# A fused attention and recurrent block: another order of TensorE's work in the attention rounds

## The chip, the cores and the metric

The kernel runs on one core of a Trainium2 chip. The metric is the time of one execution on the device in microseconds. TensorE (PE) multiplies and transposes, VectorE (DVE) and ScalarE (ACT) work on what TensorE leaves in PSUM, GpSimd (POOL) and SyncE (SP) mostly issue transfers. Each engine has its own queue of instructions, and engines wait for each other by semaphores.

## The reference

The input is x of 4 x 1024 x 1024 in float32. It is normalized over its last axis (no gain, no offset), and goes two ways, whose results are multiplied:

- Attention: queries of 16 heads, keys and values of 4 heads, 64 wide. A query sees the 512 keys up to its own position and, besides, the first four keys of the sequence (the sinks). Softmax, weighted values, a last product with Wo.
- A recurrent FFN: the last token of each sequence is normalized, passed through one layer, then four times through (norm, 1024 to 4096, gelu, 4096 to 1024, add), then through one more layer. The result is added to every token under a sigmoid gate, normalized and passed through silu.

```
att = jnp.einsum('bkgqd,bkjd->bkgqj', q, k) * scale
att = jnp.where(mask[None, None, None, :, :], att, -jnp.inf)
att = jax.nn.softmax(att, axis=-1)
y = jnp.einsum('bkgqj,bkjd->bkgqd', att, v)
...
x = x + s * g
```

## The kernel before

There are three stages, one after the other: projections of x to queries, keys, values and gates (to about 1040 us), attention (to about 1974 us), and the output product with all that follows (to the end). The change touches attention alone.

**Rounds.** Attention works in 64 rounds. Query tiles of 128 rows come in pairs (`PAIRED`, L133): a far one (tiles 7 to 4 of a sequence), whose window is full, and a near one (tiles 0 to 3), which sees 1 to 4 key tiles. A pair takes four rounds, one for each two heads' pairs of queries; `Step` (L220) holds what one tile does in one round. So the near tile has 1 key tile for four rounds, then 2, 3 and 4, and this repeats for each of the four sequences.

**One step.** `scores` (L247) multiplies queries by keys on TensorE into S. S is one tile of four PSUM banks, with no second buffer. VectorE then puts the own keys where the window has moved on (L272, far alone), adds the mask, negates and takes the minimum (L289), ScalarE takes the exponential and the sum (L294). A far step's scores are taken for one of its two queries at a time (two calls), a near step's for both at once. `normalized` (L299) scales by the reciprocal sum on VectorE. `turned` (L307) transposes one tile of 128 keys for two heads and two queries: four transposes into a PSUM tile T, of which there are two, and a copy to pT by ScalarE (L316; four buffers). For a far tile 0 VectorE also makes `lead`, its part before the window's edge (L322). `turned_sinks` (L328) does the same for the four sink columns, in 32-column pieces. `values` (L349) multiplies a turned tile by v into yp, one PSUM bank with no second buffer; `values_apart` (L356) adds sinks and lead. `stored` (L368) copies yp out on VectorE, and every second time a transfer to memory follows.

**The FFN between.** The FFN has four columns of data and 1024 KB blocks of weights, so it is cut into 173 units, a generator from L652 on, and `filler(slot)` (L847) puts the units that are due into three places of each round. A unit is mostly one block: one load, and matmuls of 32 columns (L685). The last block of a stream is followed by a copy of the sums by VectorE (L691), and the next unit turns them by four transposes (L739) into the same T tiles, which VectorE adds up (L746, L747, L751).

**Order.** TensorE's order is written out by hand (`manual_schedule` with PE alone, L856): the calls in the loop of L857 stand in its queue as they are written. The other engines' orders are chosen by the scheduler when the kernel is built, from the waits between instructions. The scores of a round are those of the next round (`far_next`, `near_next`), so that VectorE and ScalarE have time for them.

Of the kernel before, what the change touches and what calls it, by code (L numbers as in the profile page):

```python
# [43 lines left out]
def recurrent_block_kernel(  # L44
# [92 lines left out]
    sink_values, leads = {}, {}  # L137

    def load_kv(b):

        pool = pools["odd" if b % 2 else "first"]
        kT = pool.tile([P, N_KV // 2, TT, P + SINK], F32, tag="kT", name=f"kT{b}")
        v = pool.tile([P, TT, KVD], F32, tag="v", name=f"v{b}")
        for h in range(TT // BLK):
            n, at = b * (TT // BLK) + h, slice(h * BLK, (h + 1) * BLK)
            for m in range(N_KV // 2):
                nc.sync.dma_start(
                    kT[:, m, at, SINK:], k_dram[n][:, m, :].rearrange("p (t k) -> p t k", k=P)
                )
            nc.sync.dma_start(v[:, at, :], v_dram[n])  # L150
        far = WINDOW // P
        nc.gpsimd.tensor_copy(
            kT[:, :, far:, :SINK],
            kT[:, :, 0:1, SINK : 2 * SINK].to_broadcast([P, N_KV // 2, TT - far, SINK]),
        )

        sinks = pools["first"].tile([P, PAIR, KVD], F32, tag="sinks", name=f"sinks{b}", bufs=2)
        nc.gpsimd.memset(sinks, 0.0)
        for g in range(2):
            for r in range(PAIR):  # L160
                end = (2 * g + r + 1) * QUAD
                nc.gpsimd.dma_start(
                    sinks[end - SINK : end, r, :].rearrange("p (m g c) -> p m g c", m=2, g=2)[
                        :, :, g, :
                    ],
                    v_dram[b * (TT // BLK)][:SINK, 0, :].rearrange(
                        "p (m g c) -> p m g c", m=2, g=2
                    )[:, :, g, :],
                )
        kTs[b], vs[b], sink_values[b] = kT, v, sinks  # L170

    def load_q(i):
        qTs[i] = pools["first"].tile([P, N_HEAD // 2, P], F32, tag="qT", name=f"qT{i}", bufs=4)
        n, j = divmod(i, BLK)
        nc.sync.dma_start(qTs[i], q_dram[n][:, :, j * P : (j + 1) * P])
# [44 lines left out]
    class Step:  # L220
# [132 lines left out]
            last = not self.far and k + 1 == len(self.keys)  # L353
            self.added(self.pT.pop(k), vs[self.b][:, self.keys[k], :], k == 0, last)

        def values_apart(self):  # L356

            for r in range(PAIR):
                for g in range(2):
                    cols = slice((2 * self.m + g) * HS, (2 * self.m + g + 1) * HS)  # L360
                    nc.tensor.matmul(  # L361
                        self.y[g * HS : (g + 1) * HS, r * P : (r + 1) * P],
                        sink_values[self.b][:, r, cols], self.sT,
                        start=False, stop=False, skip_group_check=True,
                    )
            self.added(self.lead, leads[self.i], False, True)

        def stored(self):  # L368
# [23 lines left out]
    def steps_of(tiles, m, rp):  # L392
        return [Step(i, m, rp) for i in tiles]
# [5 lines left out]
    with ExitStack() as a:  # L399
# [193 lines left out]
        for n in range(NBLK):  # L593
# [11 lines left out]
            for kind, w7, part in (  # L605
                (queries, wq7, 0), (queries, wq7, 1), (gates, wg7, 0), (gates, wg7, 1)
            ):
                if n == NBLK - 1 and kind is gates and part == 0:
# [8 lines left out]
                    far, near = steps_of(*order[0])  # L617
# [26 lines left out]
    with ExitStack() as a:  # L644
# [188 lines left out]
        def load_y(n, row):  # L833

            t = ws.tile([P, 2, KH, BT // 2], F32, tag="stream", name=f"y2_{n}_{row}")
            ys.setdefault(n, {})[row] = t
            for j in range(BLK // 2):
                nc.sync.dma_start(
                    t[:, :, :, j * P : (j + 1) * P],
                    y_dram[n * BLK + row * (BLK // 2) + j].rearrange(  # L840
                        "p (h c q) -> p h c q", h=2, c=KH
                    ),
                )
# [3 lines left out]
        def filler(slot):  # L847
            nonlocal ffn_done
            due = FFN_UNITS * (p * SLOTS + slot + 1) // (ffn_steps * SLOTS)
            while ffn_done < min(due, FFN_UNITS + 1):  # L850
                next(ffn_gen, None)
                ffn_done += 1

        with tc.manual_schedule(engines={mybir.EngineType.PE}):  # L856
            for p in range(len(order)):  # L857
                pair, within = divmod(p, per_pair)
                if within == 0:
                    b, t = divmod(pair, TT // 2)  # L860
                    i = PAIRED[pair][0]
                    own = i % TT
                    leads[i] = px.tile([P, KVD], F32, tag="leads", name=f"leads{i}", bufs=2)
                    nc.vector.tensor_tensor(
                        leads[i], vs[b][:, own - WINDOW // P, :], vs[b][:, own, :], ALU.subtract
                    )
                    if pair + 1 < len(PAIRED):
                        for i in PAIRED[pair + 1]:
                            load_q(i)
                    if t == 1 and b + 1 < B:  # L870
                        load_kv(b + 1)


                if 0 <= p - 2 * DT < 2 * DT:
                    c, g = divmod(p - 2 * DT, 2)
                    m, r = divmod(c, GROUP)
                    h = (2 * m + g) * GROUP + r
                    tc.keep_in_program_order(
                        nc.sync.dma_start(
                            wo_sb[g * HS : (g + 1) * HS, c, :],  # L880
                            wo[h // 4, h % 2 * HS : (h % 2 + 1) * HS,
                               h // 2 % 2 * D : (h // 2 % 2 + 1) * D],
                        )
                    )
                if p > 4 * DT:
                    for dst, minuend, subtrahend in islice(wo_parts, 1):
                        tc.keep_in_program_order(
                            nc.vector.tensor_tensor(dst, minuend, subtrahend, ALU.subtract)
                        )
                if p == ffn_steps:  # L890
                    for _ in ffn_gen:
                        pass
                    for row in range(2):
                        load_y(0, row)
                more = p + 1 < len(order)
                n_near = len(near.keys)
                far.turned(0)
                far.turned_sinks()
                if more:
                    far_next, near_next = steps_of(*order[p + 1])  # L900
                    far_next.scores((0,))
                for k in (1, 2):
                    far.turned(k)
                filler(0)
                for k in range(3):
                    far.values(k)
                far.turned(3)
                if more:
                    far_next.normalized((0,))
                    far_next.scores((1,))  # L910
                for k in range(min(2, n_near)):
                    near.turned(k)
                filler(1)
                far.values(3)
                far.values_apart()
                far.stored()
                for k in range(2, n_near):
                    near.turned(k)
                if more:
                    far_next.normalized((1,))  # L920
                    near_next.scores(both)
                for k in range(n_near):
                    near.values(k)
                if more:
                    near_next.normalized(both)
                near.stored()
                filler(2)
                if more:
                    far, near = far_next, near_next

# [275 lines left out]
```

## Time and profile before

| | us |
|---|---|
| median of 3 runs | 2368.65 (2368.1 to 2369.14) |
| profiled execution | 2368.6 |
| its span, first to last instruction | 2366.9 |
| TensorE busy | 2324.0 (98%) |
| VectorE busy | 1226.0 (52%) |
| ScalarE busy | 865.4 (37%) |
| TensorE busy within 1200 to 1600 us | 392.57 of 400 |
| VectorE, ScalarE within the same | 290.91, 246.62 |

Times are from the span's start. A line of the timeline gives start, duration, engine, line of the kernel, operation, tiles written and read, shape and count; in square brackets stands for how long the engine was idle before it, and what ended that. Durations of matmuls overlap, since they are pipelined, so the distance between starts tells what one costs. A line of groups gives the count, then busy time and the mean of one in ns, then the idle time of the engine ahead of it and its releaser. TensorE's granted clock was 1.00 in every stretch read.

### The profile page before, as it was taken

How to read it: one execution, taken by the hardware profiler on the slowest of the kernel's cores; microseconds unless marked ns; L12 is line 12 of the kernel's file. 1: busy time of each engine (PE TensorE's matmuls, PEld its weight loads, DVE VectorE, ACT ScalarE, POOL GpSimd, SP SyncE). 2: the span in 40 equal slices, each digit the busy share in tenths (PEclk: the TensorE clock that was granted, in tenths of full speed). 3: DMA queues.
4: the chain of work that ended last, by engine and by line, in shares of the span. 5: the costliest groups of instructions: out<-in, count | busy, mean ns of one | idle time of the engine just before them, and what ended most of it. 6: DMA issues, size and time to landing. Idle time of an engine off the chain costs nothing.

```text
span 2366.9 us, 31507 instructions
## 1 busy us (share of the span) xinstructions
PE 2324.0 (98%) x11966; PEld 1353.1 (57%) x11966; DVE 1226.0 (52%) x2973; ACT 865.4 (37%) x1960; POOL 322.9 (14%) x480
## 2 busy tenths in 40 slices
PE   7999999999999999999999999999999999999999
PEld 5757585757576666745555555555555554444444
DVE  7222222131212211147767767777777776777776
ACT  1110101010111111056666666666656664333332
POOL 2121313121212221320001000100000000111110
PEclk9999999999999999999999999999999999999999
DMA  8243111111111111346667777667466634667563
GB/s 338 96 172 125 62 59 62 45 72 49 60 52 66 49 54 40 112 157 210 201 199 233 249 218 227 204 213 231 155 215 219 215 89 165 176 192 201 153 170 89
DMA packets 190129, 348.79 MB, mean 147 GB/s; under 512 B 10789, under 2 KB 84597, under 8 KB 188441
## 3 DMA queue, kind: packets, MB, share of 16 engines
q1 hardware_dynamic: 161448, 252.74, 33.1%
q0 software_dynamic: 23200, 74.63, 10.3%
q10 hardware_dynamic: 5328, 19.40, 2.2%
q8 instruction: 94, 1.54, 0.3%
q14 instruction: 59, 0.48, 0.1%
HBM read 271.20 MB, written 92.31 MB: 154 GB/s over the span
## 4 chain that ended last, share of the span: by engine, by line
PE 80%; issue 14%; DVE 2%; ACT 2%; DMA 1%; POOL 1%; SPq 0%; ACTq 0%; POOLq 0%; DVEq 0%
PE u_q L538 16%; PE u L1044 15%; PE u_g L559 14%; PE S L267 6%; PE yp L344 6%; PE t L312 6%; PE kp L472 5%; PE vp L461 4%; PE d_ps L685 4%; PE xtp L450 1%; PE yp L361 1%; PE st L334 1%; DMA out_beta_sb<-in_out_beta_dram 1%; ACT pr L294 1%; POOL y_dram L379 0%
## 5 line engine op out<-in xcount | busy, mean ns | idle before, releaser
L294 ACT ACTIVATE pr<-pr,nm 128x516 f32<-128x516 f32 (+4 forms) x512 | 325.3, 639 | 137.8 <-DVE nm L289 137.1
L316 ACT COPY pT<-t 128x512 f32<-128x512 f32 x416 | 230.5, 585 | 218.1 <-PE t L312 216.8
L289 DVE CUSTOM_DVE_ANT_0 pr<-S,near_mask 128x516 f32<-128x516 f32 (+4 forms) x512 | 278.2, 590 | 36.7 <-PE S L267 32.1
L267 PE MATMUL S<-kT,qT 64*128 64x512 f32 (+4 forms) x1536 | 259.7, 456 | 2.7 <-DVE nm L289 2.7
L312 PE MATMUL t<-ident,pr 128*128 128x128 f32 x1664 | 245.0, 282 | 5.6 <-ACT pT L316 3.8
L312 PEld LDWEIGHTS t<-ident,pr 128*128 128x128 f32 x1664 | 177.5, 141 | 99.1 <-issue 68.1
L344 PE MATMUL yp<-pT,v 128*64 128x256 f32 x1664 | 222.4, 391 | 2.1 <-ACT pT L316 1.8
L305 DVE TENSOR_SCALAR pr<-pr,ri 128x516 f32<-128x516 f32 (+4 forms) x512 | 199.2, 437 | 5.9
L267 PEld LDWEIGHTS S<-kT,qT 64*128 64x128 f32 x1536 | 129.6, 186 | 118.6 <-issue 100.3
L344 PEld LDWEIGHTS yp<-pT,v 128*64 128x64 f32 x1664 | 101.8, 136 | 148.1 <-issue 68.3
L538 PE MATMUL u_q<-xT,wq_sb 128*128 128x256 f32 x768 | 172.2, 379 | 0.0
L559 PE MATMUL u_g<-wg_sb,xT 128*128 128x512 f32 x384 | 171.5, 592 | 0.0
L1044 PE MATMUL u<-wo_sb,y 128*128 128x512 f32 x384 | 170.1, 592 | 1.1 <-DVE y L374 1.1
L538 PEld LDWEIGHTS u_q<-xT,wq_sb 128*128 128x128 f32 x768 | 144.8, 190 | 22.5 <-issue 3.8
L451 ACT COPY xT<-xtp 128x512 f32<-128x512 f32 x64 | 37.5, 588 | 285.2 <-PE xtp L450 285.2
L379 POOL DMA_DIRECT2D y_dram<-y x64 | 35.6, 556 | 751.2 <-DVE y L374 735.8
L1044 PEld LDWEIGHTS u<-wo_sb,y 128*128 128x128 f32 x384 | 72.9, 190 | 92.9 <-issue 91.4
L559 PEld LDWEIGHTS u_g<-wg_sb,xT 128*128 128x128 f32 x384 | 71.8, 190 | 81.4 <-issue 80.6
L566 POOL TENSOR_TENSOR t_g<-t_g,gate_b_sb 128x512 f32<-128x512 f32 x64 | 87.1, 1361 | 195.8 <-DVE t_g L513 144.0
L538 PE MATMUL u_q<-s,wq_t 128*128 128x256 f32 x512 | 113.1, 379 | 0.0
L559 PE MATMUL u_g<-wg_t,s 128*128 128x512 f32 x256 | 112.7, 593 | 0.0
L461 PE MATMUL vp<-wv_sb,xT 128*128 128x256 f32 x512 | 112.6, 380 | 0.0
(198 smaller groups left out, 2971.3 us busy)
## 6 DMA issues: line engine op xcount, KB each, us to landing
d_w<-in_d_w_dram SPq DMA_DIRECT2D x128, 1024.0 KB, 5.9
xn<-in_x_dram ACTq DMA_DIRECT2D x34, 512.0 KB, 5.0
x<-in_x_dram SPq DMA_DIRECT2D x32, 512.0 KB, 3.9
q_dram<-t_q POOLq DMA_DIRECT2D x64, 256.0 KB, 2.6
g_dram<-t_g POOLq DMA_DIRECT2D x64, 256.0 KB, 2.3
qT<-q_dram SPq DMA_DIRECT2D x32, 512.0 KB, 4.8
y_dram<-y POOLq DMA_DIRECT2D x64, 256.0 KB, 4.3
y<-y_dram SPq DMA_DIRECT2D x32, 512.0 KB, 4.6
```

What stands on the lines that cost most here:

```text
L267: nc.tensor.matmul(S[:, dst, g, at_s], qTs[self.i][half[g], at + r, :], k, start=True, stop=True,)
L289: nc.vector.tensor_tensor_reduce(out=low, in0=S[:, src, g, :cols], in1=self.mask, scale=-1.0 / HS**0.5, scalar=-NEG, op0=ALU.add, op1=ALU.min,
L294: nc.scalar.activation(low, low, AF.Exp, bias=nm, scale=-1.0, accum_out=self.sums[:, r, g : g + 1],)
L305: nc.vector.tensor_scalar(at, at, rinv[:, r, g : g + 1], None, ALU.mult)
L312: nc.tensor.transpose(ps[:, g, r, :], self.pr[g][:, r, k * P : (k + 1) * P], ident)
L316: nc.scalar.copy(self.pT[k], ps.rearrange("p g r q -> p g (r q)"))
L344: nc.tensor.matmul(self.y[g * HS : (g + 1) * HS, :], v[:, cols], pT[:, g, :], start=first, stop=last,)
L461: nc.tensor.matmul(ps[:, h, :], xT[:, c, (j + h) * P : (j + h + 1) * P], wv_sb[:, c, :], start=(c == 0), stop=(c == DT - 1),)
L472: nc.tensor.matmul(ps, wk_sb[:, c, m * P : (m + 1) * P], xT[:, c, :], start=(c == 0), stop=(c == DT - 1),)
L538: nc.tensor.matmul(bank[:, h * (BT // 2) : (h + 1) * (BT // 2)], w7[i][:, c, at], left[n][i][:, c, :], start=(first and h == 0 and c == 0) ...
L559: nc.tensor.matmul(bank, left[n][i][:, c, j * P : (j + 1) * P], w7[i][:, c, :], start=(first and c == 0), stop=(c == KH - 1), skip_group_c ...
L1044: nc.tensor.matmul(bank, left[n][i][:, c, j * P : (j + 1) * P], wo7[i][:, c, :], start=(first and c == 0), stop=(c == KH - 1), skip_group_ ...
```

## The change

The order of TensorE's work within a round is changed; no computation is added or left out. Counting as one group what stands together in TensorE's queue with one shape of operands (transposes of keys, FFN blocks and sinks in 32 columns, scores, values):

- far tiles 0 and 1 are turned together ahead of the first scores, and tiles 2 and 3 together behind the sinks; before, tile 0 stood alone, 1 and 2 together, and 3 alone.
- the first filler goes ahead of the sinks, so that two groups of 32 columns meet.
- all far values, of tiles 0 to 3, sinks and lead, stand in one group ahead of the second query's scores; before, tiles 0 to 2 stood there ahead of turning tile 3, and the rest behind the second filler. `values_apart` is cut in two, with sinks ahead of tiles 2 and 3 and the lead last. `stored` moves along, ahead of the second scores.
- the third filler joins the second where the near tile has at most two key tiles.

```diff
-        def values_apart(self):
+        def sink_values(self):
...
+        def lead_values(self):
+
             self.added(self.lead, leads[self.i], False, True)
...
-                far.turned(0)
-                far.turned_sinks()
+                for k in (0, 1):
+                    far.turned(k)
                 if more:
                     far_next, near_next = steps_of(*order[p + 1])
                     far_next.scores((0,))
-                for k in (1, 2):
+                filler(0)
+                far.turned_sinks()
+                for k in (2, 3):
                     far.turned(k)
-                filler(0)
-                for k in range(3):
+                for k in range(2):
                     far.values(k)
-                far.turned(3)
+                far.sink_values()
+                for k in range(2, 4):
+                    far.values(k)
+                far.lead_values()
+                far.stored()
                 if more:
                     far_next.normalized((0,))
                     far_next.scores((1,))
                 for k in range(min(2, n_near)):
                     near.turned(k)
                 filler(1)
-                far.values(3)
-                far.values_apart()
-                far.stored()
+                if n_near <= 2:
+                    filler(2)
                 for k in range(2, n_near):
                     near.turned(k)
...
                 near.stored()
-                filler(2)
+                if n_near > 2:
+                    filler(2)
```

The instructions are the same in kind and number: 2431 rows of TensorE's order, 1455 of ScalarE's and 2958 of VectorE's in both. The orders of ScalarE and VectorE differ too, since the scheduler chooses them anew.

## The prediction

> **What bounds the kernel now.** I read the page first, then the timeline of two rounds in the attention stage (1040 to 1974 us of the span), then the groups with their releasers.
>
> ```profile
> span 2366.9 us, 31507 instructions
> PE 2324.0 (98%) x11966; PEld 1353.1 (57%) x11966; DVE 1226.0 (52%) x2973; ACT 865.4 (37%) x1960; POOL 322.9 (14%) x480
> L316 ACT COPY pT<-t 128x512 f32<-128x512 f32 x416 | 230.5, 585 | 218.1 <-PE t L312 216.8
> ```
>
> TensorE is busy 98%; nobody it waits for stands out. So the round is as long as TensorE's own list, and other engines' delays are hidden. One round, start, duration, engine:
>
> ```profile
> 1412.59 1.56 PE L267 MATMUL S<-kT,qT 64*128 64x384 f32 x8
> 1414.08 1.51 PE L344 MATMUL yp<-pT,v 128*64 128x256 f32 x12
> 1415.53 0.66 PE L312 MATMUL t<-ident,pr 128*128 128x128 f32 x4
> 1416.12 0.43 PE L334 MATMUL st<-ident,pr 128*32 128x128 f32 x8
> 1416.47 1.35 PE L267 MATMUL S<-kT,qT 64*128 64x512 f32 x8
> 1417.83 1.09 PE L312 MATMUL t<-ident,pr 128*128 128x128 f32 x8
> 1418.86 1.07 PE L685 MATMUL d_ps<-d_w,hid_cols 128*32 128x512 f32 x8
> 1419.85 1.52 PE L344 MATMUL yp<-pT,v 128*64 128x256 f32 x12
> 1421.30 0.66 PE L312 MATMUL t<-ident,pr 128*128 128x128 f32 x4
> 1421.88 1.35 PE L267 MATMUL S<-kT,qT 64*128 64x512 f32 x8
> ```
>
> Read the starts, not the durations. Four transposes take 0.58 us to the next start, eight take 1.02: 0.109 us each, and 0.15 us per group however long it is. The same for values (1.45 us, of which 6 pairs x 0.216 = 1.30) and for the 32-column groups of FFN and sinks (1.00 against 2 x 0.429): a group costs 0.14 to 0.15 us for itself. Now the other engines beside that round:
>
> ```profile
> 1414.20 0.56 DVE L289 CUSTOM_DVE_ANT_0 pr<-S,near_mask 128x384 f32<-128x384 f32 x1 [0.97 <-PE S L267]
> 1417.34 0.18 DVE L301 RECIPROCAL ri<-s 128x4 f32<-128x4 f32 x1 [0.81 <-ACT pr L294]
> 1418.88 0.69 DVE L322 TENSOR_TENSOR lead<-pT,lead_keys 128x512 f32<-128x512 f32 x1
> 1419.48 0.43 DVE L272 COPY_PREDICATED S<-own_keys,S 128x256 f32<-128x256 uint32 x1
> 1420.68 0.73 ACT L294 ACTIVATE pr<-pr,nm 128x516 f32<-128x516 f32 x1 [1.02 <-DVE nm L289]
> 1421.40 0.71 ACT L294 ACTIVATE pr<-pr,nm 128x516 f32<-128x516 f32 x1
> 1422.12 0.56 ACT L316 COPY pT<-t 128x512 f32<-128x512 f32 x1
> ```
>
> From the first near reduction (1414.20) to the end of the two exponentials of the next far query (1422.11) is an unbroken dependence of 7.91 us: near reductions, near exponentials, near scaling, lead product, replaced keys, far reductions, exponentials. The copy of turned tile 3 starts only then, though its transposes were through by 1421.96. It delays nobody, since its values (tile 3) are issued at 1425.19.
>
> **What the change saves on TensorE.** In the built order of both kernels I counted groups of one shape in the attention stage: 870 before, 688 after. Transposes 287 to 233, 32-column groups 200 to 136 (FFN and sinks share a shape, and meet), values 192 to 128; scores stay 189. So 54 x 0.15 + 64 x 0.14 + 64 x 0.15 = 26.7 us: per round 0.58 us where near has 1 or 2 key tiles, 0.44 us where it has 3 or 4. No matmul is added or dropped. The trace is weighed here against the Trainium skill, page "TensorE: Matmul & The Clock Gate", Part 2: weight loads are pulled ahead of running matmuls, so back-to-back spacing is the moving length alone. By that a group costs nothing and the saving is 0; the row above shows 0.15 us, and I take the row.
>
> **What it exposes.** All far values now stand together, so values of tiles 2 and 3 are wanted earlier, and the second query's scores stand behind them. In ScalarE's built order the line before was copy 0, sinks, copies 1 and 2, two exponentials, copy 3. After, in 38 of 63 rounds, it is copies 0 and 1, sinks, two exponentials, then copies 2 and 3 (form A); in 17 only copy 3 is behind them (B); in the others neither, or mixed (C). The same page, Part 1 (the paragraph on queue depths), calls ACT and DVE strict FIFO; the copy at 1422.12 behaves so. With that rule the sum below holds; if copies could pass waiting exponentials, the result would be the 26.7 us gain, about 2342.
>
> Behind the waiting values on TensorE stand the lead values, the store of y and then the second query's scores S1; and S1 starts the next pass. Worked from the timeline for 3 near tiles, from S1's start: its exponentials wait for two near copies and it is scaled by 5.64 (1421.88 to 1427.52, the y copy between the two scalings taken out, as it moves ahead of them); near reductions follow at 5.67; 7.91 later the far exponentials end; copies 2 and 3 take 0.57 + 0.50 and 0.05 to be seen; tile 3's and lead values are 4 pairs, 4 x 0.216 + 0.15 = 1.01; then the next S1. That is 5.67 + 7.91 + 1.12 + 1.01 = 15.7 us. TensorE's own list after the saving is 15.53 - 0.44 = 15.1, so it would stand still some 0.5 us at tiles 2 and 3. For other sizes the first term is 5.3 with one near tile (one copy ahead), 5.67 with two, 6.35 with four (the near scores end last), the second 6.25, 7.08 and 8.95, read in the same way. Form B saves the second copy, 0.5 us, but with three near tiles gives it back, as copy 2 delays the exponentials.
>
> - 1 near tile: before 12.86, list alone 12.3, A 13.7, B 13.2
> - 2 near tiles: before 14.11, list alone 13.5, A 14.9, B 14.4
> - 3 near tiles: before 15.53, list alone 15.1, A 15.7, B 15.7
> - 4 near tiles: before 16.80, list alone 16.4, A 17.4, B 16.9
>
> Rounds of form A: 10, 11, 8 and 7 of these sizes: 10 x 0.84 + 11 x 0.79 + 8 x 0.17 + 7 x 0.6 = +22.7. Form B 3, 3, 7, 4: 0.3 x 6 + 0.17 x 7 + 0.1 x 4 = +3.4. C, eight: -0.5 each, -4. That is +22: the saving of 26.7 is in it, so the waits cost about 49.
>
> **Further terms.** FFN turned rows (L739) at slot 0 take a bank of the two for transposes; now sinks and tile 2 come right behind and tile 2 needs that bank, which VectorE frees (L747) only behind both far reductions. In 6 rounds that is some 1.3 us more: +8. Slots 1 and 2 stand together where near has 1 or 2 tiles; in 6 rounds these are the last FFN block and its turned rows, with VectorE's copy of 0.7 us (L691) between, of which 0.4 us lands on the pass: +2.5. The Gelu table loads stand in ScalarE's queue 4 times; before, the row of exponentials ended 1.4 to 2.4 us late in those rounds and TensorE did not notice; now about 1 us each: +4. Bounds for all three: 0 (all inside the same standing time) and 30; I take 14, as each sits on an engine of the pass. The 8 us that TensorE now loses between transposes and sinks (bank not free) may vanish: in the range, not in the sum. DMAs: none added; weights for F are asked for when the block four earlier is through, more than a round ahead, and land in 5.9 us (median), at most about 10; with slots 1 and 2 together that still fits, cost 0, and 0.3 us a round if it did not. SP's and POOL's queues keep their issues. Stages before 1040 and after 1974 us are unchanged.
>
> Sum: +22 + 14 = +36 on the profiled 2368.6 us (span 2366.9 and 1.7 around it), which is the median of the runs to 0.1: **2405 us**.
>
> **Rivals.** (1) *Faster*: the far exponentials end early enough that copies 2 and 3 are never late. It decides when the 7.91 us is at least 0.6 us shorter with three near tiles and 1.4 with two. The scaling of the near tiles would have to be quicker than the trace has it; nothing in the built order says so. Then 2368.6 - 26.7 = 2342, with the bank waits gone 2334. Chance 0.10. (2) *Balanced*: waits as large as the saving, since delays of one round give slack to the next; forms B and C speak for it, and three near tiles is nearly even. 2364 to 2385. Chance 0.08. (3) *Worse*: the FFN chains, with slots 1 and 2 together, add to the pass each time (34 turned rows or layer-norm steps x 1 us), 2435 or more. Chance 0.08. That the change does not do what it says is excluded: the groups are fewer in the built order. The likeliest, 2385 to 2435 with 2405 in it, has 0.74.
>
> **Range.** A change under 0.2% (4.7 us) can't be told from none. Faster 0.10, same 0.05 (most of the balanced case), slower 0.85. The range 2372 to 2435 leaves out the faster case, the low part of the balanced one and the worse one, 0.2 in all.
>
> **What would show it.** Right: TensorE's share of busy time in 1100 to 1900 us falls from 98% to about 94%; waits of yp (L344) for the copy pT appear, about 40 us in all; copies 2 and 3 follow the exponentials at once; periods between second-query scores of 13.7, 14.9, 15.7 and 17.4. Group steps still 0.58 and 1.02. Wrong: yp never waits, and rounds of 13.5 and 15.1 us, or waits mainly at the transposes.

## The result: slower by 1.7%, and the profile after

The changed kernel takes 2409.8 us (2408.56 to 2410.66) where the kernel before takes 2368.5 us: a ratio of 1.0173, 95% interval 1.0161 to 1.0186. Forecast were 2405 us and "slower". The profiled execution of the changed kernel took 2410.66 us with a span of 2408.9, 42.0 us more than the span before.

Where the 42 us are: from the first transpose of the attention to its last values, 934.2 us have become 973.5 (+39.3). The last stage is 2.7 us longer, and the first is unchanged (the attention starts at 1039.7 in both). The page of the changed kernel, busy times and the two groups that matter:

```profile
span 2408.9 us, 31475 instructions
PE 2320.1 (96%) x11966; PEld 1362.9 (57%) x11966; DVE 1226.6 (51%) x2973; ACT 857.6 (36%) x1960; POOL 321.6 (13%) x480
L344 PE MATMUL yp<-pT,v 128*64 128x256 f32 x1664 | 227.0, 394 | 31.2 <-ACT pT L316 31.1
L312 PE MATMUL t<-ident,pr 128*128 128x128 f32 x1664 | 238.0, 283 | 14.4 <-ACT sT L339 5.0
```

TensorE does the same 11966 matmuls and is busy for 4 us less, yet the span is longer: time has gone into standing still. The group of the values (yp) names who it stands still for, ScalarE's copies of turned tiles. The waits of TensorE's matmuls, sorted by what ended them (us in total, times, longest), show it next to everything else. First the row of before for the values, then the first rows of the changed kernel:

```profile
PE yp L344 <- ACT pT L316: 1.8, 1, 1.8
```

```profile
PE yp L344 <- ACT pT L316: 31.1, 45, 1.6
PE xtp L453 <- DVE x L116: 11.7, 1, 11.7
PE d_tr L742 <- DVE d_sb L694: 5.4, 6, 0.9
PE t L312 <- ACT sT L339: 5.0, 8, 2.3
PE t L312 <- ACT pT L316: 4.1, 9, 0.7
```

Of the changed kernel's rows, the second lies in the first stage and was there before. The first is new but for the 1.8 us. The third is new too: the FFN's turned rows (d_tr) now follow their last block at once and wait for VectorE's copy of it. In the fourth, 2.3 us are one wait in the first round of the attention. The stretch from 1100 to 1900 us of the span, before and then now (length, then busy time of PE, PEld, DVE, ACT, POOL, then the granted clock):

```profile
1100.00:1900.00 800.00, 786.58 (x6336) 426.64 (x6336) 583.66 (x1890) 494.87 (x1287) 39.68 (x69) 1.00 0.67 213
1100.00:1900.00 800.00, 746.54 (x6071) 414.24 (x6067) 560.70 (x1818) 467.56 (x1236) 38.63 (x68) 1.00 0.63 206
```

TensorE's share has fallen from 98% to 93%, at full clock in both. One pass of the mechanism in the timeline, with 3 near tiles (start, duration, engine):

```profile
1426.79 1.11 PE L312 MATMUL t<-ident,pr 128*128 128x128 f32 x8
...
1427.47 0.72 ACT L294 ACTIVATE pr<-pr,nm 128x516 f32<-128x516 f32 x1 [0.28 <-DVE nm L289]
1427.83 1.08 PE L344 MATMUL yp<-pT,v 128*64 128x256 f32 x8
...
1428.19 0.71 ACT L294 ACTIVATE pr<-pr,nm 128x516 f32<-128x516 f32 x1
1428.75 0.61 PE L361 MATMUL yp<-sT,sinks 128*64 128x128 f32 x8
...
1428.90 1.05 ACT L316 COPY pT<-t 128x512 f32<-128x512 f32 x2
...
1429.52 1.14 PE L344 MATMUL yp<-pT,v 128*64 128x256 f32 x8 [0.17 <-ACT pT L316]
1430.49 0.60 PE L344 MATMUL yp<-lead,leads 128*64 128x256 f32 x4
1431.02 1.35 PE L267 MATMUL S<-kT,qT 64*128 64x512 f32 x8
```

Tiles 2 and 3 are turned by 1427.9. ScalarE could copy them then, but two exponentials stand ahead in its queue until 1428.9. The sinks take 0.43 us from start to start where nothing is awaited, so the values of tiles 2 and 3 could have started at 1429.18; they start at 1429.52, with ScalarE's pT as releaser. The lead values and the second query's scores at 1431.02 stand behind them. Here, with 3 near tiles, the delay is 0.34 us; there are 45 such waits in the list above, the longest of 1.6 us.

### The profile page after: what moved, and what is told of

It reads as the page before. It is cut to its first block, busy times and chain, and to the rows that moved or that the text cites. A ratio compares the mean times of both kernels' runs of the same rounds, so it can differ in the third digit from the quotient of the medians.

```text
span 2408.9 us, 31475 instructions
## 1 busy us (share of the span) xinstructions
PE 2320.1 (96%) x11966; PEld 1362.9 (57%) x11966; DVE 1226.6 (51%) x2973; ACT 857.6 (36%) x1960; POOL 321.6 (13%) x480
## 4 chain that ended last, share of the span: by engine, by line
PE 68%; issue 14%; ACT 8%; DVE 7%; DMA 1%; POOL 1%; SPq 0%; ACTq 0%; POOLq 0%; DVEq 0%
PE u_q L541 16%; PE u L1053 15%; PE u_g L562 14%; ACT pr L294 5%; PE kp L475 5%; PE vp L464 4%; PE S L267 4%; PE yp L344 4%; PE t L312 3%; DVE pr L305 2%; DVE pr L289 2%; PE d_ps L688 2%; ACT pT L316 2%; PE xtp L453 1%; DVE lead L322 1%
## 5 line engine op out<-in xcount | busy, mean ns | idle before, releaser
L316 ACT COPY pT<-t 128x512 f32<-128x512 f32 x416 | 224.1, 580 | 216.4 <-PE t L312 216.3
L344 PE MATMUL yp<-pT,v 128*64 128x256 f32 x1664 | 227.0, 394 | 31.2 <-ACT pT L316 31.1
L312 PE MATMUL t<-ident,pr 128*128 128x128 f32 x1664 | 238.0, 283 | 14.4 <-ACT sT L339 5.0
L1053 PE MATMUL u<-wo_t,s 128*128 128x512 f32 x256 | 112.5, 592 | 0.0
```

Source lines behind the costliest of these rows:

```text
L312: nc.tensor.transpose(ps[:, g, r, :], self.pr[g][:, r, k * P : (k + 1) * P], ident)
L316: nc.scalar.copy(self.pT[k], ps.rearrange("p g r q -> p g (r q)"))
L344: nc.tensor.matmul(self.y[g * HS : (g + 1) * HS, :], v[:, cols], pT[:, g, :], start=first, stop=last,)
L1053: nc.tensor.matmul(bank, left[n][i][:, c, j * P : (j + 1) * P], wo7[i][:, c, :], start=(first and c == 0), stop=(c == KH - 1), skip_group_ ...
```

## The experiments

Two measures are used below beside the times. The *attention* is the stretch from the first transpose to the last values in the profiled execution. *Standing still* is what is left there when from each step between two matmul starts the usual step of that shape is taken off; the rest is TensorE's *list*. Both come from the starts in the trace:

| kernel | groups | attention | standing still | list |
|---|---|---|---|---|
| before | 870 | 934.2 | 29.1 | 905.1 |
| changed | 688 | 973.5 | 85.6 | 887.9 |
| far exponentials ahead of copies 2 and 3, everywhere | 688 | 998.3 | 108.3 | 889.9 |
| copy 2 ahead, copy 3 behind, everywhere | 688 | 974.8 | 86.4 | 888.4 |
| both copies ahead, everywhere | 688 | 929.1 | 47.2 | 882.0 |
| values of tiles 2 and 3 put back | 760 | 932.0 | 41.3 | 890.7 |
| before, with far values together only | 781 | 980.8 | 81.6 | 899.2 |

The split into list and standing still is good to some 8 us only: the four kernels with 688 groups issue the same matmuls in the same order, so their lists ought to be equal, and they differ by as much. With one set of usual steps for all kernels together, their list comes out some 20 us shorter than before (0.11 a group). The attention's length, 934.2 and the others, does not depend on this split.

My theory: the values of far tiles 2 and 3 wait for copies that stand in ScalarE's queue behind the next far query's exponentials, and the second query's scores, which start the next pass through VectorE and ScalarE, wait behind those values. The rival: the FFN slots that now stand together, or the score group, make the delay.

**ScalarE's order alone.** Three kernels differ from the changed one only in where ScalarE issues the two far exponentials: ahead of copies 2 and 3, between them, or behind both, in all 63 rounds. TensorE's order is that of the changed kernel: its matmuls stand in the same order in the four traces, and VectorE's order differs from the changed kernel's by at most four of 2973 instructions.

```diff
-                    far_next.scores((0,))
+                    far_next.scores((0,), later=True)
                 filler(0)
                 far.turned_sinks()
                 for k in (2, 3):
                     far.turned(k)
+                if more:
+                    far_next.exponentials(True)
```

This is the form behind both: `later=True` keeps the two exponentials back, and `exponentials(True)` issues them at that place and holds them in program order. In the other two forms the call stands ahead of `turned(2)` or between `turned(2)` and `turned(3)`, and the copies after it are held in program order too.

Ahead, everywhere:

> The changed kernel, TensorE's order untouched; on ScalarE the two far exponentials are pinned ahead of copies 2 and 3 in all 63 rounds (the changed kernel has this in 38). Theory (the pass: exponentials, copies 2 and 3, last values, next scores): the 17 rounds of form B gain up to 0.5 us each except with 3 near tiles, the 8 of form C 0.5 to 2: 2420 us (2412 to 2428). Rival (the copies' place in ScalarE's queue is not what the rounds wait for, the loss comes from the grouping itself or from the FFN units that stand together): 2410 within 4.

Measured: 2434.5 us (2434.05 to 2439.8), ratio 1.0281 (1.0266 to 1.0297). The direction is as expected, the size larger than the range. Nine rounds have neither form A nor form B in the changed kernel's trace; they became 18.8 us longer in all, the last three by 2.5 to 3.4 us each, where 0.5 to 2 had been given for each of eight.

Between, everywhere:

> The same with copy 2 ahead of the two exponentials and copy 3 behind them in all rounds. Theory: 28 rounds of form A lose their 0.5 us, rounds with 3 near tiles stay, the 8 of form C get slower: 2402 us (2394 to 2410). Rival: 2410 within 4.

Measured: 2412.8 us (2409.57 to 2414.56), ratio 1.0183 (1.0168 to 1.0198). It lies 3 us above the range, and is no better than the changed kernel, which mixes the forms. It is also within the rival's range, so this run by itself does not tell the two apart; the runs on both sides of it do.

Behind, everywhere:

> The same with copies 2 and 3 both ahead of the two exponentials in all rounds. Theory: values never wait for a copy; what is left is TensorE's own list, 26.7 us shorter than before, plus waits around FFN units that the long rounds had covered in part (turned rows behind the last block, 6 x 1 us; bank of tile 2 at slot 0, 6 x 1.3; layer norm steps and first round about 8): 2358 us (2345 to 2370), and waits of yp for pT under 5 us where the changed kernel has 31. Rival: 2410 within 4.

Measured: 2364.2 us (2361.63 to 2366.34), ratio 0.9978 (0.9969 to 0.9987), as expected, and faster than both kernels. The waits of TensorE in the kernel with the exponentials ahead, first lines:

```profile
PE yp L355 <- ACT pT L325: 50.1, 55, 2.3
...
PE d_tr L753 <- DVE d_sb L705: 5.4, 6, 0.9
```

and in the one with the exponentials behind both copies:

```profile
PE xtp L462 <- DVE x L116: 11.5, 1, 11.5
PE t L321 <- ACT pT L325: 5.9, 11, 1.0
PE d_tr L751 <- DVE d_sb L703: 5.4, 6, 0.9
PE st L343 <- ACT pT L325: 3.2, 4, 1.3
```

Same matmuls in the same order, 70 us apart, and the only row that comes and goes by more than 5 us is yp's wait for pT: 50.1 us there, not in the list here (xtp is the first stage's row). The FFN's row d_tr, 5.4 us, is the same in both. The transposes' waits (t) change little but their releaser: for pT 5.9 us here and 1.9 there, for VectorE's adding of the FFN's turned rows (hid_cols) none here and 4.8 there. So the order of two instruction kinds in ScalarE's queue decides between a loss of 66 us and a gain of 4 or 5.

**The FFN slots.** The third FFN slot, which the change puts beside the second where there are 1 or 2 near tiles, goes back to the round's end. ScalarE's order stays pinned with both copies ahead.

```diff
                 filler(1)
-                if n_near <= 2:
-                    filler(2)
...
-                if n_near > 2:
-                    filler(2)
+                filler(2)
```

> As the one before, and the third filler always at the round's end, as before the change (undoes one part). Theory: some 24 groups more at 0.14 us, +3.4, and six waits of 1 us for the sums of the last FFN block gone, -6: 2355 us (2342 to 2367). Rival (the FFN units that stand together are the cause of the loss): 2345 or less, at least 12 under the run before.

Measured: 2373.8 us (2371.72 to 2378.91), ratio 1.0023 (1.0014 to 1.0032): a miss. The FFN units standing together are worth 9.5 us to the kernel, where I had them cost time. The attention is 8.3 us longer, of which TensorE's list accounts for 1.8 us and standing still for 6.4. The two rows of TensorE's waits that grew most:

```profile
PE S L268 <- DVE nm L290: 8.7, 16, 1.9
...
PE t L321 <- DVE hid_cols L759: 7.5, 6, 1.4
```

Without the FFN block between, the near scores come before VectorE is through with the reductions of the scores that occupy their bank (16 waits, 8.7 us, against 2.4 us with the slots together). And where the FFN's turned rows stand at the round's end, the next round's first transposes wait for the bank until VectorE has added the rows up (7.5 us, none with the slots together); the 5.4 us of d_tr are gone in exchange. In this kernel the joined slots give cover and cost nothing, against the rival. For the changed kernel itself the next two runs decide it: the first keeps the joined slots and loses nothing, the second has none and loses as much.

**Undoing the values.** In the changed kernel, with ScalarE's order left to the scheduler, only this goes back: values of tiles 2 and 3, the lead values and the store of y stand behind the second query's scores and the FFN units.

```diff
                 far.sink_values()
-                for k in range(2, 4):
-                    far.values(k)
-                far.lead_values()
-                far.stored()
...
                 filler(1)
                 if n_near <= 2:
                     filler(2)
+                for k in range(2, 4):
+                    far.values(k)
+                far.lead_values()
+                far.stored()
```

> The changed kernel with one part undone: values of far tiles 2 and 3, lead values and the store of y stand again behind the second query's scores, the near transposes and the FFN units; transposes, sinks, score group and joined FFN slots stay as changed. ScalarE's order is left as built, and is still exponentials ahead of copies 2 and 3 in 36 of 63 rounds, copy 3 alone behind in 17. My theory: the copies are as late as before, but nobody wants them so early, so yp's waits for pT fall from 31 us to under 5, and 64 groups come back (9.6 us): 2371 us (2360 to 2382). A middle outcome, the near transposes wait for the banks of tiles 2 and 3 instead: 2385 to 2400. Rival, the cause is the joined FFN slots, the score group or the transposes, which all stay: 2400 or more.

Measured: 2366.5 us (2364.54 to 2367.49), ratio 0.9988 (0.9982 to 0.9995), within the range. This is the run that names the part. The exponentials are still ahead of both copies in 36 rounds; every other part of the change is in, and all of the 41 us lost come back, with 2 more (2409.8 to 2366.5). Its group of the values:

```profile
L344 PE MATMUL yp<-pT,v 128*64 128x256 f32 x1664 | 223.0, 392 | 1.4 <-DVE y L377 1.2
```

No wait for pT is left in that row, and none was moved to the transposes (their waits for pT are 2.2 us in all, 4.1 in the changed kernel). A late copy is harmless while nobody wants it.

**The values alone.** The converse: to the kernel before, only the far values together are added, with the transposes of tile 3 ahead of them. FFN slots, score group and the first transposes stay.

```diff
-                for k in range(3):
-                    far.values(k)
                 far.turned(3)
+                for k in range(4):
+                    far.values(k)
+                far.values_apart()
+                far.stored()
                 if more:
                     far_next.normalized((0,))
...
                 filler(1)
-                far.values(3)
-                far.values_apart()
-                far.stored()
```

> The kernel before with one part of the change alone: all far values, sinks, lead values and the store of y stand together, ahead of the second query's scores; transposes of tile 3 come behind the FFN unit, ahead of the values; FFN slots, score group and first transposes as before. ScalarE's order: in 57 of 63 rounds copy 2, then both exponentials, then copy 3. 64 groups fewer on TensorE, so by its list alone 2359 us. My theory: the values wait for copy 3 behind the exponentials, as they do in the kernel with copy 2 pinned ahead and copy 3 behind (waits of yp for pT 35 us there, typical rounds 13.0, 14.3, 15.6 and 16.9): these rounds against 12.9, 14.1, 15.4 and 16.8 before make 2381 us (2372 to 2395), with yp waits for pT of 20 us or more. Rival, values together are harmless and it takes the joined FFN slots or the score group to make the wait: 2357 to 2366, yp waits under 5 us.

Measured: 2414.8 us (2414.51 to 2415.19), ratio 1.0195 (1.0178 to 1.0212). The theory has the direction and the wait, but the size is three to four times what I gave. Its waits:

```profile
PE yp L344 <- ACT pT L316: 26.2, 39, 1.7
...
PE t L312 <- ACT pT L316: 9.3, 17, 2.4
```

and the end of one pass in its timeline:

```profile
1429.73 0.56 ACT L316 COPY pT<-t 128x512 f32<-128x512 f32 x1
...
1430.83 0.61 PE L361 MATMUL yp<-sT,sinks 128*64 128x128 f32 x8
1431.26 0.60 PE L344 MATMUL yp<-lead,leads 128*64 128x256 f32 x4
1431.79 1.35 PE L267 MATMUL S<-kT,qT 64*128 64x512 f32 x8
```

The second row is a bank wait: tile 3's transposes come earlier, and need a bank that a copy frees. In the timeline only one copy is late, but the sinks (0.43 us from start to start) stand behind tile 3 too, so the scores start 1.50 us after the copy's end; in the changed kernel, where the sinks go ahead of tile 2, it is 1.07 us after the second copy's (1429.95 to 1431.02). The typical round was mis-sized too: the medians are 13.5, 14.7, 15.5 and 17.3 us for 1 to 4 near tiles, where 13.0, 14.3, 15.6 and 16.9 had been taken. Over the rounds that is some 19 of the 34 us missing in the expectation. How these 19 us divide between the bank wait and the place of the sinks, and where the rest lies, was not measured.

**A dose of VectorE.** If the pass through VectorE and ScalarE sets the round, more work on it must be seen; if TensorE's list does, it must be hidden. The lead product (L322, about 0.69 us) is made twice in three kernels: exponentials ahead, exponentials behind both copies, and before. The dose is 63 x 0.69 = 43 us in each, none of it on TensorE.

```diff
+                for _ in range(2):
                     nc.vector.tensor_tensor(
                         self.lead.rearrange("p g (r q) -> p (g r) q", r=PAIR),
```

> The kernel with both exponentials pinned ahead of copies 2 and 3 in all rounds (2434.5 us), with VectorE's lead product (0.69 us) made twice; same result, 63 times 0.69 us more on VectorE, nothing more on TensorE. My theory: the product lies on the pass that sets the round, so nearly all of it is seen: 2475 us (2465 to 2480). Rival, VectorE's chain has slack and the late copies come from something else: under 2445.

Measured: 2469.8 us (2467.79 to 2470.95), 35.3 us more than without the dose: 81% of it is seen.

> The kernel with copies 2 and 3 pinned ahead of the exponentials in all rounds (2364.2 us), with the lead product made twice. My theory: the pass through VectorE no longer ends in TensorE's next scores, so the same 43 us on VectorE are mostly hidden: 2367 us (2363 to 2377). Rival, VectorE's chain bounds this kernel too: 2400 or more.

Measured: 2369.2 us (2366.49 to 2371.48), 4.9 us more: 11%.

> The kernel before, with VectorE's lead product (0.69 us) made twice in every round. My theory: before the change the far exponentials had 1.4 us or more of room behind them, so the 43 us on VectorE are nearly all hidden: 2372 us (2368 to 2380), with no wait of yp for pT above 5 us in all. Rival, VectorE's chain already set the round before the change: 2395 or more.

Measured: 2372.0 us (2370.87 to 2374.0), ratio 1.0012 (1.0005 to 1.0018), 2.9 us more: 7%. All three as expected. In the first, this row of the waits says where the dose came out:

```profile
PE yp L356 <- ACT pT L325: 76.7, 56, 2.8
```

yp's waits for pT went from 50.1 to 76.7 us. A product on VectorE has lengthened a wait for ScalarE's copy: the copy is only the last link of that pass.

**What is left to mend.** Two placements of the FFN's turned rows are changed in the kernel with both copies ahead: at slot 0 they go behind the first two values instead of ahead of the sinks and tile 2, and they no longer follow the last block in a joint slot. `ends` is true where the FFN unit before was the last block of a stream.

```diff
-                filler(0)
+                turn = ends
+                if not turn:
+                    filler(0)
...
                 for k in range(2):
                     far.values(k)
+                if turn:
+                    filler(0)
...
-                if n_near <= 2:
+                joined = n_near <= 2 and not ends
+                if joined:
                     filler(2)
...
-                if n_near > 2:
+                if not joined:
                     filler(2)
```

> The same pinned kernel (2364.2 us), with two placements of the FFN's turned rows mended: where they fall on slot 0 they come behind the far transposes and the first two values, and where they would follow the last FFN block of the same joint slot, slot 2 goes to the round's end. My theory: the six waits of turned rows for VectorE's copy (5.4 us) and most of the waits of tile 2 for a bank (some 4 to 6 us) go, for up to 12 groups more (1.8 us): 2356 us (2350 to 2361). Rival, these waits only move to the next place: 2363 to 2367.

Measured: 2362.3 us (2358.86 to 2364.9), ratio 0.9968 (0.9956 to 0.9979): a miss, 1.9 us better than without, not 8, and the runs of the two kernels overlap, so that even this gain is not clear of the noise. Both waits did go (d_tr for d_sb 5.4 to nothing, t for pT 5.9 to 1.9 us), but a new one stands in the list:

```profile
PE t L321 <- DVE hid_cols L759: 7.5, 6, 1.4
```

VectorE adds up the turned rows behind other work, and now the transposes wait for that bank. So in the next kernel, for 1 or 2 near tiles, the turned rows stand between the near scores and the near values.

```diff
                     near_next.scores(both)
+                if not joined and n_near <= 2:
+                    filler(2)
...
-                if not joined:
+                if n_near > 2:
                     filler(2)
```

> The pinned kernel with the FFN's turned rows mended (2362.3 us), where turned rows had stood at a round's end with the next round's first transposes right behind; six waits of these for VectorE's adding of the turned rows (hid_cols, 7.5 us in all) were seen there. Now, with 1 or 2 near tiles, they stand between the near scores and the near values, so that the bank has 1.7 to 3.5 us more to come free. My theory: 5 us or more of these waits go, for up to 6 groups more (0.8 us): 2358 us (2355 to 2361). Rival, VectorE frees the bank behind the near reductions, and the wait only moves: 2361 to 2366.

Measured: 2356.3 us (2355.72 to 2357.5), ratio 0.9949 (0.9932 to 0.9965), the fastest of all. The time is as expected, the reason only in part: the hid_cols waits fell from 7.5 to 6.0 us, not by 5, so most of them are not the ones I moved. In the profiled executions, 6.8 us apart, the attention is 2.9 us shorter, but the last stage, which the edit does not touch, is shorter by 3.6: there the earlier kernel had 6.8 us at half clock (below) and this one none. So at most 3 us of the gain can be the edit's, and in the attention too there are 3.4 us less at half clock, an estimated 1.7 us. How much is left for the moved rows is open.

## Why the prediction was right

**The saving on TensorE: right in kind, too large.** 182 groups fewer were to save 26.7 us. With the exponentials behind both copies the list is 905.1 - 882.0 = 23.1 us shorter by the table, 0.127 us a group where 0.14 to 0.15 had been read, and some 20 us by the common steps. The kernel with the values put back has 72 groups more than that one and a list 8.7 us longer, 0.12 each. So the saving is real, as the row had it, and not the 0 that the prediction worked out from the Trainium skill's account of weight loads pulled ahead of running matmuls ("TensorE: Matmul & The Clock Gate", Part 2). The same part also says, of the back-to-back gap, that in a stream of loads and matmuls both set the spacing, so the 0 was read from half of it; the measurement decides. The 17.2 us that the table gives for the changed kernel itself differ from this by the error of the split. One sum of the prediction does not fit its own total: 0.58 and 0.44 us a round would be 32.6 us over 64 rounds, not 26.7, so its column "list alone" is on average too low.

**The waits: right in place and form.** "What it exposes" is confirmed from both sides. Take the exponentials away from ahead of the copies, and yp's waits vanish (2364 us); take the demand away, and they vanish too (2366 us); add the demand alone to the kernel before, and they appear (2415 us). The forecast was "about 40 us in all": the list of waits has 31.1, and from the starts 38.9 us are lost inside groups of values, 36.9 more than before. TensorE's busy share fell to 93%, where about 94% was forecast. The strict order of ScalarE's queue, which the same page states in Part 1, is what the pinned kernels show with 70 us between the two ends.

**The pass: right to 0.2 us.** Medians from one second-query scores to the next, over all rounds of a size:

| near tiles | before | forecast, form A | changed, form A | changed, all |
|---|---|---|---|---|
| 1 | 12.86 | 13.7 | 13.62 | 13.53 |
| 2 | 14.06 | 14.9 | 14.75 | 14.75 |
| 3 | 15.34 | 15.7 | 15.58 | 15.58 |
| 4 | 16.80 | 17.4 | 17.42 | 17.36 |

For before with 2 and 3 near tiles the prediction had 14.11 and 15.53, which is what one gets by counting a period to the near tile of the round in which it begins; the table counts it to the round in which it ends. The dose shows that these links are the pass: 81% of an added delay on VectorE comes out in the time where the exponentials are ahead.

**The sum by forms: right in all, shifted inside.** Against the same round before, rounds of form A lost 25.7 us (22.7 forecast), form B 12.2 (3.4), and the others gained 0.6 (4). Form B was the term that was mis-sized. Its periods were close to the forecast with 1 and 2 near tiles (13.51 and 14.76 against 13.2 and 14.4), but I measured its loss against the median before of all rounds, and just those rounds had been shorter before (with 3 near tiles 14.63 against 15.34). The pinned kernel with form B everywhere says the same: at 2412.8 us it is not the milder form that I took it for. These sums hold the further terms as well, since FFN work falls in rounds of all forms: 22 + 14 = 36 was forecast, and 37.3 is the sum over the rounds.

**The further terms: there, in part.** The six waits of turned rows behind their last block are in the list, six times, 5.4 us, with VectorE's copy as releaser; 2.5 had been put down. Without them and the bank waits the kernel with both copies ahead gained only 1.9 us, as VectorE's adding of the rows came next: these terms are real but don't add up. The largest, 8 us for tile 2's bank, can't be found: waits for VectorE's adding of the turned rows (hid_cols and th) were 4.0 us before, at the sinks, and are 2.7 now, at the transposes. The Gelu loads were not tried apart. What was not forecast: the first round is 3.2 us longer, with one wait of 2.3 us for the sinks' copy, which stands behind the exponentials there, and a stretch at half clock; and the last stage is 2.7 us longer, though it was to be unchanged. One of its products waits 2.9 us for VectorE, where the longest such wait was 1.2 before, and TensorE then runs into 3.4 us at half clock.

So the mechanism was right, but that the total fits to 5 us is in part luck. The forms together lost 15 us more than the 22 forecast for them, the further terms of 14 us are found only to about 5, and the first round and the last stage were in no sum.

**The rivals.** "Faster" needed exponentials early enough for the copies; with the copies pinned ahead the kernel reached 2364 us, not 2342, since standing still of 47 us, 18 more than before, eats most of the 23 us saved. So even with its cause removed, the change would not have given the gain in the sum by TensorE's list. "Balanced", 2364 to 2385, needed waits no larger than the saving, and they were larger by 41 us. "Worse" by the FFN chains falls with the run that takes the slots apart and gets slower, and with the one that keeps them joined and loses nothing.

## What to carry to other kernels

Moving consumers together pays only if their producers are not queued behind other work: before bringing a matmul forward, look at what stands ahead of its operand's copy in the producer's in-order queue, in the built order, and at who stands behind the matmul. Here some 20 us saved on TensorE's list came with 56 us more of standing still, and one pinned order on ScalarE turned a loss of 41 us into a gain of 4. A dose of known size on the suspected chain (81% seen, against 7 to 11% where TensorE was the bound) tells within one run which of two loops sets the round.

## What the runs showed of the hardware that was not expected

The granted clock of TensorE fell to half for stretches of 3.413 us, or twice that. The profile of before has none within its work; that of the changed kernel has four, beginning at 1046.5, 1056.7, 1305.9 and 2036.3 us of its span. Each begins within 2 us of a moment in which TensorE had been idle for 0.8 to 2.9 us. Before, idle times of 1.4 and 1.8 us passed without one, and so did three of 1.5 to 1.6 us in the changed kernel, where idle times of 0.8 us and more are common, so the length of the idle time alone does not decide. The Trainium skill ("TensorE: Matmul & The Clock Gate", Part 1) has the clock fall after an idle window of about 3.4 us; the length of the stretches agrees, 3.413 us, but no idle time before them was that long. A window over the first two of them in the changed kernel (granted clock third from the end):

```profile
1040.00:1060.00 20.00, 15.68 (x105) 9.49 (x105) 11.02 (x42) 12.33 (x31) 5.11 (x9) 0.83 0.90 304
```

A stretch costs at most 1.7 us, half its length, and the four some 7 us in all: an estimate from their lengths. Which of them the change brings about was not tried; the kernels with the smallest standing still in their attention did not all have the fewest.
